# Two attention blocks on one core: reciprocals sent to their rows over DRAM, and a sum of score quarters moved into an earlier phase

## The chip, the core and the metric

The kernel runs on one core of a Trainium2 chip. The engines named below are PE (TensorE, matrix products), DVE (VectorE), ACT (ScalarE), POOL (GpSimd) and SP (SyncE, which issues most of the transfers). The metric is the device time of one execution in microseconds; less is better. The data are float32 throughout.

## The reference

Two layers follow each other on x of shape (8, 512, 32, 32), that is 8 samples of 512 channels and 1024 positions. Layer 0 is attention with 8 heads of 64 channels behind a group norm; layer 1 is attention with one head of 512 channels behind a norm over the whole sample. Cut to what matters:

```python
# layer 0
h = group_norm(x, norm_w, norm_b)
q, k, v = qkv of h, split into 8 heads of 64
attn = softmax(einsum('bhnd,bhmd->bhnm', q, k) / sqrt(64))
o = einsum('bhnm,bhmd->bhnd', attn, v)
x = x + proj_w @ o + proj_b
# layer 1
n = norm of x over a whole sample
q, k, v = wq @ n + bq, wk @ n + bk, wv @ n + bv
attn = softmax(einsum('bci,bcj->bij', q, k) * 512 ** -0.5)
out = einsum('bcj,bij->bci', v, attn)
x = x + wo @ out + bo
```

## The kernel before

The eight samples are computed one after another, each in some 348 us. The order of instructions on PE, ACT and DVE is the order of the program text, written out by hand; the order on POOL and SP is left to the planner of the language. A helper, `at_steps`, runs a generator of matrix products and calls other work (hooks) after its step of a given number, and `together` takes steps from several generators in turn. So a hook's number decides where DVE's work stands in DVE's queue.

Larger matrix products are made by Strassen's scheme in Winograd's form (seven products for eight): `strassen` uses one PSUM bank called `line` and one called `single`, and sums of input quarters with names such as S1 to S4 and T1 to T4. Some products apply the scheme twice.

**Softmax sums of layer 0.** The scores are exponentiated without their maximum. The heads lie two in a tile, so there are four pairs, in the order 0, 2, 1, 3. The sums over keys are gathered in tiles `acc` on DVE (L780). Pairs are joined in couples: couple one is pairs 0 and 2, couple two pairs 1 and 3. After a pair, `fold` moves half of its sums by three transfers (L1039 to L1041). `sum_couple` (L1054) multiplies by ones, so that each head's sum of a half of the positions (g = 0 or 1, 512 positions) stands in a block of 32 partitions, the same number in each. `one_over_couple` (L1065) takes the reciprocals on DVE and sends them to the partitions of their heads: each tile `spreads[pair]` needs, for each half g, the values of two heads on 64 partitions each, so the block of 32 partitions is copied twice for each head. These are eight transfers of 32x512 for each half, issued by SP (L1072). `divide` (L960) multiplies the outputs `o` by the tile. Couple one does this inside the attention of couple two. Couple two does it beside the query and key products of the next sample's layer 0 (`pairs_qk`), by the hooks 3 to 9; behind the last `divide` stand four differences (`combine2`, L1010) and then the projection (`project`, L1163), whose add L1183 empties the bank `single` before PE fills it again. In the last sample the couples are not used; there the rows go by `spread` (L801).

**Scores of layer 1.** The 1024x1024 scores are four quarters of 512x512, C11, C12, C21 and C22; the tile of the quarter in row j and column i of keys and queries is `ps[j][k][i]`, k being which half of its keys. The seven products of the outer scheme are made in three phases:

- phase one: the products that go to several quarters, and P5 (`twice("S1", "T1", ...)`), which is put into `ps[1][k][1]`;
- phase two: `twice("A12", "B21", ...)` on the banks of tag o for C11, beside `twice("S3", "T3", ...)` on the banks of tag s, which completes what C12 and C22 share and puts it into `ps[0][k][1]`;
- phase three: `twice("S4", "B22", ...)` for one quarter and `twice("A22", "T4", ...)` for another.

`twice` applies the scheme a second time inside, so it has seven steps. Each step has two matmuls into the bank `line` or `single`, and an add (or copy) of that bank into a quarter of a tile (L1335 on DVE). A bank is filled again two steps later, and must have been read by then. Steps of the two `twice` of a phase alternate.

Two sums over whole tiles of 128x1024 complete the quarters, both in `with_p5` (L1378): `ps[1][k][0] += ps[1][k][1]` for each k (hooks 14 in phase one and 3 in phase two), and C22, `ps[1][k][1] += ps[0][k][1]`, in `c22(k)`, followed by the exponential (L1299): k = 0 after phase two, k = 1 at hook 3 of phase three. POOL meanwhile makes sums for the values (`sum_v`, L1429), parts of the softmax sums (`add_up`, L1294 and L1296) and second sums for the products of values (`halve_v`, `halve_p`).

Of the kernel before, what the change touches and what calls it, by code (L numbers as in the profile page):

```python
# [37 lines left out]
FP = mybir.dt.float32  # L38
AF = mybir.ActivationFunctionType
ALU = mybir.AluOpType  # L40
# [6 lines left out]
P = 128  # L47
# [4 lines left out]
HALF = 512  # L52
HD = 64
# [12 lines left out]
def two_attention_blocks(  # L66
# [17 lines left out]
    nc = tc.nc  # L84
# [5 lines left out]
    dram = ctx.enter_context(tc.tile_pool(name="dram", bufs=1, space=bass.MemoryType.DRAM))  # L90
# [7 lines left out]
    def banks(tag, name):  # L98
        return psum.tile([P, 2, HALF], FP, tag=tag, name=name)

    def tile2(name):
        return tpool.tile([P, 2, HALF], FP, tag="t", name=name)
# [377 lines left out]
    def sums_b(q, ts, engine=nc.vector):  # L480

        q.update({f"T{i + 1}": t for i, t in enumerate(ts)})
        for n, x, y in [(1, "B12", "B11"), (2, "B22", "T1"), (3, "B22", "B12"), (4, "B21", "T2")]:
            engine.tensor_tensor(q[f"T{n}"], q[x], q[y], ALU.subtract)
        return q
# [101 lines left out]
    def together(*groups):  # L587

        groups = list(groups)
        spares.clear()  # L590
        while groups:
            for g in list(groups):
                if next(g, g) is g:
                    groups.remove(g)
                else:
                    yield
        spares.clear()
# [289 lines left out]
    def layer0(bs, qs, ks, b, norm_next):  # L887
# [24 lines left out]
        accs, sums, invs, spreads = {}, {}, {}, {}  # L912
# [50 lines left out]
        ps = {}  # L963
# [99 lines left out]
            held(ps_couple[g], f"sum_{name}", invs[g])  # L1063

        def one_over_couple(couple, g):  # L1065
            nc.vector.reciprocal(invs[g], invs[g])  # L1066
            for n, pair in enumerate(couple):
                if g == 0:
                    spreads[pair] = tile2(f"inv_{b}_{pair}")
                for j in range(2):  # L1070
                    for r in range(2):
                        nc.sync.dma_start(  # L1072
                            spreads[pair][(j * 2 + r) * 32 : (j * 2 + r + 1) * 32, g, :],
                            invs[g][(n * 2 + j) * 32 : (n * 2 + j + 1) * 32, :],
                        )

        def held_couple(g):
            held(invs.pop(g), f"inv_{b}_{g}")
# [10 lines left out]
        def couple_steps(i):  # L1089
            if ended(i - 1) is not None:  # L1090
                fold(ended(i - 1))
            if ended(i - 5) is not None:
                folded(ended(i - 5))
            couple = couples[0]
            if ended(i - 7) == couple[1]:
                ps_sum = banks("o", f"ps_sum_{b}_{couple[0]}")
                sum_couple(couple, [ps_sum[:, g, :] for g in range(2)])
            for g, (at_copy, at_over, at_held, at_divide) in enumerate([(7, 8, 14, 13), (8, 10, 18, 15)]):
                if ended(i - at_copy) == couple[1]:
                    copy_couple(couple, g)  # L1100
                if ended(i - at_over) == couple[1]:
                    one_over_couple(couple, g)
                if ended(i - at_held) == couple[1]:
                    held_couple(g)
                if ended(i - at_divide) == couple[1]:
                    divide_couple(couple, g)

        last = norm_next is None
        for i in range(2, len(units) + 2):
# [6 lines left out]
            pair, g, kt = units[i - 5] if i >= 5 else (None, None, None)  # L1116
            name = f"0_{b}_{pair}_{g}"
# [8 lines left out]
            pair, g, kt = units[i - 9] if i >= 9 else (None, None, None)  # L1126
            if pair in invs and kt == NT - 1:
                held(invs.pop(pair), f"inv_0_{b}_{pair}_{g}")
            pair, g, kt = units[i - 10] if i >= 10 else (None, None, None)
# [3 lines left out]
        if b == 0:  # L1133
            rows, = throughs
# [3 lines left out]
        if not last:  # L1138


            couple = couples[1]
# [67 lines left out]
    def attention1(xs, norm, b, at_values):  # L1209

        last = b + 1 == B
# [18 lines left out]
        def halve_a(name, t=None, engine=nc.vector):  # L1230
            q = {f"A{n}": v for n, v in halve(q_parts[name], lambda i, j: (j, i)).items()}
            twice_a[name] = sums_a(q, flat(tile2(f"{name}_twice_{b}")) if t is None else t, engine)
# [51 lines left out]
        ps = [[[tile2(f"p_1_{b}_{j}{k}{i}") for i in range(2)] for k in range(2)] for j in range(2)]  # L1284
# [3 lines left out]
        def add_up(j, k, i):  # L1288

            engine = nc.vector if i else nc.gpsimd  # L1290
            for u in range(2):
                seen[i].append(ps[j][k][i][:, u, :])
                if len(seen[i]) == 2:
                    engine.tensor_tensor(acc[:, i, :], *seen[i], ALU.add)  # L1294
                elif len(seen[i]) > 2:
                    engine.tensor_tensor(acc[:, i, :], acc[:, i, :], seen[i][-1], ALU.add)  # L1296

        def exp_of(p):
            nc.scalar.activation(p, p, AF.Exp, scale=norm.factor)  # L1299
# [13 lines left out]
                    nc.scalar.copy(to[:, t % 2, :], bank)  # L1313
                yield

        def twice(a, v, tags, i, j, fresh, final):

            a, v = twice_a[a], twice_b[v]  # L1320
            line, single = (banks(tag, f"ps_{n}_1_{b}_{i}{j}")[:, 0, :] for tag, n in zip(tags, "ls"))

            def multiply(bank, x, y, start):
                for u in range(2):
                    nc.tensor.matmul(  # L1325
                        bank[:, u * 2 * P : (u + 1) * 2 * P], v[y][:, u * P : (u + 1) * P], a[x],
                        start=start and u == 0, stop=True, skip_group_check=True,
                    )

            def at(r, t):  # L1330
                return ps[j][t][i][:, :, r * 2 * P : (r + 1) * 2 * P]

            def add(bank, r, t):
                bank = bank.rearrange("p (u q) -> p u q", u=2)
                nc.vector.tensor_tensor(at(r, t), bank, at(r, t), ALU.add)  # L1335

            def take(bank, r, t):
                if fresh:
                    nc.scalar.copy(at(r, t), bank.rearrange("p (u q) -> p u q", u=2))
                else:  # L1340
                    add(bank, r, t)

            def done(r, t):
                if final:
                    exp_of(at(r, t))
                    if i == 0 and (r, t) in ((0, 1), (1, 0)):
                        add_up(j, t, i)

            multiply(line, "A11", "B11", True)
            take(line, 0, 0)  # L1350
            yield
            multiply(single, "A12", "B21", True)
            add(single, 0, 0)
            done(0, 0)
            yield
            multiply(line, "S2", "T2", False)
            take(line, 0, 1)
            yield
            multiply(single, "S1", "T1", True)
            take(single, 1, 1)  # L1360
            yield
            multiply(line, "S3", "T3", False)
            add(line, 1, 1)
            done(1, 1)
            yield
            multiply(single, "S4", "B22", False)
            add(single, 0, 1)
            done(0, 1)
            yield
            multiply(line, "A22", "T4", False)  # L1370
            take(line, 1, 0)
            done(1, 0)
            yield

        def with_p5(i, j, k):

            to, other = ps[j][k][i], ps[1][k][1] if i == 0 else ps[0][k][1]
            nc.vector.tensor_tensor(to, to, other, ALU.add)  # L1378

        def c22(k):  # L1380
            with_p5(1, 1, k)
            exp_of(ps[1][k][1])


        spare = wpool.tile([P, W_SIZE], FP, tag="w", name=f"spare_{b}")
# [2 lines left out]
        def halve_t3():  # L1388
# [3 lines left out]
            together(  # L1392
                in_turn(together(line(0), line(1)), together(line(2), line(3))),
                twice("S1", "T1", "oo", 1, 1, True, False),
            ),
            {
                2: [lambda: halve_a("A12", spare[0])], 5: [lambda: halve_a("S3", spare[1])],
                8: [halve_t3], 14: [lambda: with_p5(0, 1, 0)],
            },
        )  # L1400
        halve_a("S4", None, nc.gpsimd)
# [29 lines left out]
        for n in range(1, 3):  # L1431
            sum_v(n, nc.gpsimd)
        at_steps(
            together(
                twice("A12", "B21", "oo", 0, 0, False, True), twice("S3", "T3", "ss", 1, 0, False, False)
            ),
            {3: [lambda: with_p5(0, 1, 1)]},
        )
        c22(0)


        twice_v, twice_p = {}, {}
# [8 lines left out]
        def halve_p(name, engine):  # L1451
            q = {
                f"B{i + 1}{j + 1}": p_parts[i][name][:, :, j * 2 * P : (j + 1) * 2 * P]
                for i in range(2) for j in range(2)
            }
            ts = [tile2(f"{name}_p_twice_{b}_{i}") for i in range(2)]
            sums = [t[:, i, :].rearrange("p (u q) -> p u q", u=2) for t in ts for i in range(2)]
            twice_p[name] = sums_b(q, sums, engine)

        if not last:  # L1460
# [2 lines left out]
            together(  # L1463
                twice("S4", "B22", "oo", 0, 1, False, True), twice("A22", "T4", "ss", 1, 0, False, True)
            ),
            {3: [lambda: c22(1)], 5: [] if last else [lambda: halve_p("B22", nc.gpsimd)]},
        )

        for n in range(1, 5):
# [14 lines left out]
        invs, later = [], []  # L1484
# [685 lines left out]
```

## Time and profile before

| | |
|---|---|
| median of 3 runs | 2840.18 us (2839.46 to 2842.13) |
| the profiled execution | 2839.93 us |
| its span, first to last instruction | 2838.1 us |
| granted TensorE clock | 1.000 |
| scores, phases two and three, first sample (334 to 362 us): busy PE, DVE, ACT, POOL | 27.83, 24.05, 11.15, 23.82 us of 28 |
| reciprocal 128x512 on DVE (L1066), 28 times | 3346 ns each |
| sum over 128x1024 in `with_p5` (L1378), 32 times | 1215 to 2158 ns, median 1836 |
| add of a bank into a quarter (L1335) | 683 and 684 ns |
| issue of a transfer of the reciprocals (L1072), 224 times | 507 to 1708 ns, median 589 |
| landing of such a transfer | median 2.0 us |
| write of layer 1's reciprocals to DRAM (L1562), 8 times | issue 550 ns |
| read of them for all partitions (L1564), 8 times | issue 339 ns, landing 3.6 us |

A busy share says how long an engine had an instruction in hand. PE's instructions overlap and their ends are modelled, so PE's share doesn't show short delays; they are read from the starts of its matmuls in order of time. An instruction that waits keeps what stands behind it on its own engine waiting too; so the order on an engine matters as much as its load.

### The profile page before, as it was taken

What the parts mean: (1) busy time and instruction counts of PE and PEld (TensorE: products, weight loads), DVE (VectorE), ACT (ScalarE), POOL (GpSimd) and SP (SyncE); (2) the same over time, 40 slices, a digit from 0 to 9 for tenths busy, and PEclk for the clock granted to TensorE, in tenths of its full rate; (3) what the DMA queues carried; (4) which work ended last, traced back from release to release, by engine and by line L of the source; (5) the groups of instructions that cost most, each with busy time, mean ns of one, the idle gap of its engine ahead of it and who ended that gap; (6) DMA issues with size and microseconds to landing.
All of it is one profiled execution on the core that took longest, in us unless ns stands there. A gap on an engine that the chain in (4) does not pass through costs nothing.

```text
span 2838.1 us, 38370 instructions
## 1 busy us (share of the span) xinstructions
PE 2825.0 (100%) x15328; PEld 1518.4 (53%) x15328; DVE 2124.3 (75%) x2891; ACT 1118.0 (39%) x1564; POOL 273.6 (10%) x236
## 2 busy tenths in 40 slices
PE   9999999999999999999999999999999999999999
PEld 5434765347643476435773356733567335673365
DVE  6686696867867678777777777777777777767867
ACT  3462324623256232553325522265232642326432
POOL 0000220003100040000400004000040000400011
PEclk9999999999999999999999999999999999999999
DMA  8512132121322213213132131322213222121001
GB/s 289 179 42 74 58 121 94 42 89 53 111 93 50 86 70 107 80 46 108 56 108 79 40 106 56 108 79 46 100 59 105 79 56 90 63 85 57 8 16 39
DMA packets 81227, 228.90 MB, mean 81 GB/s; under 512 B 20080, under 2 KB 20880, under 8 KB 74640
## 3 DMA queue, kind: packets, MB, share of 16 engines
q1 hardware_dynamic: 76576, 210.61, 23.0%
q10 hardware_dynamic: 4464, 15.76, 1.7%
q8 instruction: 122, 2.00, 0.3%
q14 instruction: 65, 0.53, 0.1%
HBM read 157.35 MB, written 30.70 MB: 66 GB/s over the span
## 4 chain that ended last, share of the span: by engine, by line
PE 91%; DVE 6%; issue 1%; SPq 1%; DMA 0%; ACT 0%; POOL 0%; DVEq 0%; POOLq 0%
PE s L921 16%; PE ps_o L940 15%; PE ps_q L612 10%; PE ps_v L627 7%; PE ps_o L1489 7%; PE ps_p L612 5%; PE ps_l L1325 4%; PE ps_s L1308 4%; PE ps_k L612 3%; PE ps_l_v L627 3%; PE ps_s L1325 3%; PE ps_l_qk L849 3%; PE ps_s_v L870 2%; PE ps_s_two L1619 2%; PE ps_s_qk L842 2%; PE ps_o_v L870 1%
## 5 line engine op out<-in xcount | busy, mean ns | idle before, releaser
L778 ACT ACTIVATE p<-s 128x1024 f32<-128x1024 f32 x512 | 524.0, 1025 | 322.1 <-PE s L921 308.3
L780 DVE TENSOR_TENSOR acc<-acc,p 128x1024 f32<-128x1024 f32 x384 | 469.2, 1222 | 99.4 <-ACT p L778 86.3
L940 PE MATMUL ps_o<-p,v 64*64 64x512 f32 x4096 | 528.6, 589 | 0.0
L940 PEld LDWEIGHTS ps_o<-p,v 64*64 64x64 f32 x4096 | 156.6, 133 | 282.8 <-issue 278.9
L921 PE MATMUL s<-q,k 64*64 64x512 f32 x2304 | 298.5, 591 | 0.0
L921 PE MATMUL s<-c_q,c_k 64*64 64x512 f32 x1792 | 233.0, 590 | 0.0
L339 POOL TENSOR_TENSOR rstd<-rstd,minus_half 128x4 f32<-128x4 f32 (+1 forms) x16 | 19.8, 1239 | 2087.7 <-DVE rstd L338 2087.7
L921 PEld LDWEIGHTS s<-q,k 64*64 64x64 f32 x2304 | 86.3, 133 | 162.6 <-issue 156.6
L1489 PE MATMUL ps_o<-t_p,s_v 128*128 128x512 f32 x384 | 168.2, 594 | 0.0
L921 PEld LDWEIGHTS s<-c_q,c_k 64*64 64x64 f32 x1792 | 67.7, 133 | 126.3 <-issue 114.9
L780 DVE TENSOR_TENSOR acc<-p,p 128x1024 f32<-128x1024 f32 x64 | 77.9, 1217 | 73.5 <-ACT p L778 73.5
L1299 ACT ACTIVATE p<-p,factor 128x512 f32<-128x512 f32 (+1 forms) x112 | 85.3, 780 | 115.7 <-DVE p L1335 91.2
L1313 ACT COPY p<-ps_s 128x512 f32<-128x512 f32 x96 | 53.1, 588 | 177.1 <-PE ps_s L1308 177.1
L1489 PEld LDWEIGHTS ps_o<-t_p,s_v 128*128 128x128 f32 x384 | 72.3, 190 | 91.3 <-issue 89.2
L1335 DVE TENSOR_TENSOR p<-ps_l,p 128x512 f32<-128x512 f32 x136 | 90.0, 683 | 41.0 <-PE ps_l L1325 40.7
L612 PE MATMUL ps_p<-t_p,w_p 128*128 128x512 f32 x256 | 114.8, 597 | 2.4 <-DVE u_p L1183 1.3
L612 PE MATMUL ps_q<-t,w_wqk 128*128 128x512 f32 x256 | 116.0, 597 | 0.0
L425 ACT COPY u_q<-ps_q 128x512 f32<-128x512 f32 x75 | 43.6, 581 | 177.1 <-PE ps_q L612 177.1
L1066 DVE RECIPROCAL inv<-inv 128x512 f32<-128x512 f32 x28 | 93.7, 3346 | 22.9 <-ACT inv L788 22.9
L425 ACT COPY u_v<-ps_v 128x512 f32<-128x512 f32 x48 | 28.1, 586 | 204.9 <-PE ps_v L627 185.9
L1335 DVE TENSOR_TENSOR p<-ps_s,p 128x512 f32<-128x512 f32 x112 | 74.8, 684 | 37.9 <-PE ps_s L1325 37.9
L627 PE MATMUL ps_v<-w_v,t_again 128*128 128x256 f32 x448 | 99.0, 379 | 0.0
(457 smaller groups left out, 4903.5 us busy)
## 6 DMA issues: line engine op xcount, KB each, us to landing
x<-in_x SPq DMA_DIRECT2D x92, 512.0 KB, 6.8
w_qk<-stored_qk SPq DMA_DIRECT2D x14, 1792.0 KB, 7.3
inv<-inv SPq DMA_DIRECT2D x248, 64.0 KB, 2.0
w_wqk<-stored_wqk SPq DMA_DIRECT2D x8, 1792.0 KB, 7.6
fold<-acc SPq DMA_DIRECT2D x56, 256.0 KB, 3.1
w_wvo<-stored_wvo SPq DMA_DIRECT2D x8, 1792.0 KB, 7.5
out<-x SPq DMA_DIRECT2D x28, 512.0 KB, 3.3
w_v<-stored_v SPq DMA_DIRECT2D x7, 1792.0 KB, 7.1
```

Source lines behind the costliest of these rows:

```text
L612: nc.tensor.matmul(bank, w[a][:, k, c * P : (c + 1) * P], bs[b][:, k, :], start=fresh and k == 0, stop=k == 1, skip_group_check=True,)
L627: nc.tensor.matmul(bank[:, u * 2 * P : (u + 1) * 2 * P], bs[b][:, k, n * P : (n + 1) * P], w[a][:, k, :], start=fresh and u == k == 0, sto ...
L778: nc.scalar.activation(p, s, AF.Exp, scale=factor)
L780: nc.vector.tensor_tensor(acc, first, p, ALU.add)
L921: nc.tensor.matmul(s[cols, j, :], ks[pair][k0 // HALF][rows, k0 % HALF : k0 % HALF + HD], qs[pair][g][rows, :], start=True, stop=True,)
L940: nc.tensor.matmul(o[cols, half, :], vs[kt][rows, c0 : c0 + HD], p[rows, j, :], start=kt == 0, stop=kt == NT - 1,)
L1066: nc.vector.reciprocal(invs[g], invs[g])
L1299: nc.scalar.activation(p, p, AF.Exp, scale=norm.factor)
L1308: nc.tensor.matmul(bank, bs[v][:, k, t * P : (t + 1) * P], q_parts[a][:, k, :], start=a == "A11" and k == 0, stop=k == 1, skip_group_check ...
L1325: nc.tensor.matmul(bank[:, u * 2 * P : (u + 1) * 2 * P], v[y][:, u * P : (u + 1) * P], a[x], start=start and u == 0, stop=True, skip_group ...
L1335: nc.vector.tensor_tensor(at(r, t), bank, at(r, t), ALU.add)
L1489: nc.tensor.matmul(bank, v_parts[kt // 2][a][:, kt % 2, c * P : (c + 1) * P], p_parts[kt // 2][b][:, kt % 2, cols], start=fresh and kt == ...
```

## The change

It has two parts.

In layer 0, each half of a couple's reciprocals is written to DRAM as four rows of 512 (one for each head, from the first partition of each block of 32), and read back by two transfers, one for each pair, which put two rows on 64 partitions each. So there are three transfers for each half in place of eight; the two reads wait for the write to land. Nothing else of `one_over_couple` changes, and its hooks stay.

In layer 1, `c22` no longer sums whole tiles. `twice` gets an argument `also`, called in its inner `done` for each finished quarter; `twice("S3", "T3", ...)` in phase two passes `c22`, which adds that quarter of `ps[0][t][1]` to the same quarter of `ps[1][t][1]` and exponentiates it. So C22 is complete with phase two, as four sums of 128x512 in place of two of 128x1024, and four exponentials in place of two. The sum of the other whole tile (`with_p5(1)`), which must read P5 before C22 is added to it, moves from hook 3 to hook 2 of phase two. In phase three, hook 3 goes, and `halve_p("B22")` on POOL moves from hook 5 to hook 2.

```diff
         def one_over_couple(couple, g):
             nc.vector.reciprocal(invs[g], invs[g])
+            rows = dram.tile([4, HALF], FP, tag=f"inv_{g}", name=f"inv_rows_{b}_{couple[0]}_{g}")
+            nc.sync.dma_start(rows, invs[g][0:P:32, :])
             for n, pair in enumerate(couple):
                 if g == 0:
                     spreads[pair] = tile2(f"inv_{b}_{pair}")
-                for j in range(2):
-                    for r in range(2):
-                        nc.sync.dma_start(
-                            spreads[pair][(j * 2 + r) * 32 : (j * 2 + r + 1) * 32, g, :],
-                            invs[g][(n * 2 + j) * 32 : (n * 2 + j + 1) * 32, :],
-                        )
+                nc.sync.dma_start(
+                    spreads[pair][:, g, :],
+                    rows[n * 2 : (n + 1) * 2, :].unsqueeze(1).to_broadcast([2, HD, HALF]),
+                )
...
-        def twice(a, v, tags, i, j, fresh, final):
+        def twice(a, v, tags, i, j, fresh, final, also=None):
...
             def done(r, t):
+                if also is not None:
+                    also(r, t)
                 if final:
                     exp_of(at(r, t))
...
-        def with_p5(i, j, k):
-            to, other = ps[j][k][i], ps[1][k][1] if i == 0 else ps[0][k][1]
-            nc.vector.tensor_tensor(to, to, other, ALU.add)
-
-        def c22(k):
-            with_p5(1, 1, k)
-            exp_of(ps[1][k][1])
+        def with_p5(k):
+            nc.vector.tensor_tensor(ps[1][k][0], ps[1][k][0], ps[1][k][1], ALU.add)
+
+        def c22(r, t):
+            to, c21 = (ps[j][t][1][:, :, r * 2 * P : (r + 1) * 2 * P] for j in (1, 0))
+            nc.vector.tensor_tensor(to, to, c21, ALU.add)
+            exp_of(to)
...
-                8: [halve_t3], 14: [lambda: with_p5(0, 1, 0)],
+                8: [halve_t3], 14: [lambda: with_p5(0)],
...
-                twice("A12", "B21", "oo", 0, 0, False, True), twice("S3", "T3", "ss", 1, 0, False, False)
+                twice("A12", "B21", "oo", 0, 0, False, True), twice("S3", "T3", "ss", 1, 0, False, False, c22)
             ),
-            {3: [lambda: with_p5(0, 1, 1)]},
+            {2: [lambda: with_p5(1)]},
         )
-        c22(0)
...
                 twice("S4", "B22", "oo", 0, 1, False, True), twice("A22", "T4", "ss", 1, 0, False, True)
             ),
-            {3: [lambda: c22(1)], 5: [] if last else [lambda: halve_p("B22", nc.gpsimd)]},
+            {2: [] if last else [lambda: halve_p("B22", nc.gpsimd)]},
         )
```

## The prediction

> **What bounds the kernel now.** I read the page first, then the order of time on PE, DVE, POOL and SP around the two places that the change touches, in each of the eight samples.
>
> ```profile
> PE 2825.0 (100%) x15328; PEld 1518.4 (53%) x15328; DVE 2124.3 (75%) x2891; ACT 1118.0 (39%) x1564; POOL 273.6 (10%) x236
> ...
> inv<-inv SPq DMA_DIRECT2D x248, 64.0 KB, 2.0
> ...
> inv<-inv_rows SPq DMA_DIRECT2D x8, 512.0 KB, 3.6
> ```
>
> PE is never idle for long. Its 128x512 matmul is two records 0.43 us apart, its 128x256 one two records 0.215 us apart; whenever a record starts later than that, PE was held. I added these delays up: 48 us in the whole span, so no edit that leaves the matmuls alone can bring more. A delay has two parts: the wait, and some 0.107 us after it, because the next group also starts that much late. Only two places concern us.
>
> Place one is the projection of layer 0 (fifth sample, order of time; start and duration in us, in brackets the idle time before and who ended it):
>
> ```profile
> 1629.69 11.84 SPq L1072 DMA_DIRECT2D inv<-inv  x16
> ...
> 1632.10 3.34 DVE L1066 RECIPROCAL inv<-inv 128x512 f32<-128x512 f32 x1
> ...
> 1643.06 0.69 DVE L960 TENSOR_TENSOR o<-o,inv 128x512 f32<-128x512 f32 x1 [1.80 <-DMA inv<-inv]
> ...
> 1646.94 3.23 PE L612 MATMUL ps_p<-t_p,w_p 128*128 128x512 f32 x6 [0.72 <-DVE u_p L1183]
> ```
>
> SP issues sixteen transfers one by one for 11.84 us, the last divide (L960) waits 1.80 us for one of them, and behind it in DVE's order stand four differences (L1010) and the add (L1183) that PE waits for. Wait plus restart at this place and the like one 2 us later, by sample: 0.27, 0.25, 0.24, 0.68, 1.38, 0.75, 1.29; together 4.87 us. The eighth sample divides in another way and is not touched.
>
> Place two is the second and third phase of layer 1's scores (first sample; DVE, POOL and PE in order of time: start, duration, both in us):
>
> ```profile
> 342.15 2.15 DVE L1378 TENSOR_TENSOR p<-p,p 128x1024 f32<-128x1024 f32 x1
> 344.22 1.28 DVE L1335 TENSOR_TENSOR p<-ps_l,p 128x512 f32<-128x512 f32 x2
> ...
> 354.73 2.09 DVE L1378 TENSOR_TENSOR p<-p,p 128x1024 f32<-128x1024 f32 x1
> 356.74 1.27 DVE L1335 TENSOR_TENSOR p<-ps_l,p 128x512 f32<-128x512 f32 x2
> ```
> ```profile
> 339.48 2.50 POOL L1429 TENSOR_TENSOR s_v<-c_v,c_v 128x512 f32<-128x512 f32 x2
> 341.94 3.49 POOL L1429 TENSOR_TENSOR s_v<-s_v,c_v 128x512 f32<-128x512 f32 x2
> ```
> ```profile
> 343.93 1.03 PE L1325 MATMUL ps_s<-spare 128*128 128x256 f32 x4
> 344.95 1.13 PE L1325 MATMUL ps_l<-spare,B_twice 128*128 128x256 f32 x4
> ...
> 356.28 1.03 PE L1325 MATMUL ps_s<-A_twice,T_twice 128*128 128x256 f32 x4
> 357.47 1.13 PE L1325 MATMUL ps_l<-S_twice,B_twice 128*128 128x256 f32 x4 [0.17 <-DVE p L1335]
> ```
>
> A turn of PE (two matmuls, four records) is 0.86 us. Call the turns of the two streams A1, B1, A2, B2 and so on to A7, B7. Each fills a bank that is used again four turns later, so DVE's add of A3 must end before A5 starts. At 343.93 to 344.95 it came 0.16 us late, at 356.28 to 357.47 0.33 us late, both times behind a whole-tile sum of L1378. With restarts: second phase 0.27, 0, 0.26, 0.28, 0.28, 0.27, 0.26 (1.62 us), third phase 0.44 in each of seven samples (3.04 us). The eighth has neither.
>
> **What the Trainium skill says.** (1) "GPSIMD Engine Reference", Specifications: GpSimd shares its SBUF interfaces with VectorE and contends with DVE instructions that have two SBUF inputs. The trace agrees: L1378 takes 1.22 us alone and up to 2.16 beside POOL, the POOL sum then waiting takes 2.27 instead of 1.27, while L1335, which has one input in PSUM, stays at 0.68 to 0.69 beside POOL. (2) "Perfetto Trace Analysis", Optimizing Scalar/DVE Operations: where DVE is not saturated but causes bubbles elsewhere, smaller instructions may finish work sooner. Here the second phase is close to saturated, see below. (3) "DMA: Bandwidth & Descriptors", Anatomy of one DMA: a transfer has a fixed cost of about 2 us, mostly the receipt. Landing of 2.0 us for 64 KB agrees.
>
> **Part 1, reciprocals over DRAM.** Removed: 224 issues at 0.59 us (8 for each of 28 halves). Added: 28 writes of 8 KB, 56 row reads of 256 KB. The trace has the like for layer 1 (write of 4 KB, one read of 512 KB): the read is issued 1.8 us after the write's issue began, its issue takes 0.34 us, and it lands after 3.6. For a half: 0.1 + 1.8 + 2 x 0.34 + at most 3.6 = 6.2 us after its reciprocal; if half the size lands in 2.5, 5.1. Now: the second reciprocal ends at 1635.44, its last row lands at 1643.06, that is 7.6 us (6.5 in the first sample). The last divide then comes at 1640.5 to 1641.6, a lead of 1.4 to 2.5 us in the fifth sample and 0.3 to 1.4 us in the first (242.49 to 249.0 now). The delays to be covered are, without restarts, 0.88 + 0.29 and 0.17, and one restart that falls away moves PE by 0.1. So all are covered, and I take the full 4.9 us. More is excluded, as nothing else of PE hangs on these rows: the rows of the first two head pairs arrive far inside the attention, where no PE delay names them. What is late next is DVE's add of a bank that PE has itself just filled, which has its usual slack. SP waits some 1.1 us for each write (8.6 us for eight in layer 1 now); behind it stands the load of w_wvo, which waits for PE until about the same time anyway. Ends of the cost: -4.9 to 0, should the reads land as late as the rows do now.
>
> **Part 2, C22 by quarters.** Matmuls are the same. DVE loses the two sums at the head of the third phase (1.25 and 2.09 us there) and gets four of 128x512 in the second; the second whole-tile sum comes one add earlier, before B2. Four quarters at 0.68 (L1010: 128x512, two SBUF inputs) are 2.7 us. Load of DVE in the second phase: 14 adds at 0.60 (pairs of them start 1.20 apart; 8.4) + 1.22 + 2.7 = 12.3 us against 14 turns of 0.86 = 12.1, before any wait for POOL. In the third it falls to 8.4 us, so its 3.04 us of delay goes.
>
> The order up to A3's add is now A1, B1, A2, whole sum, B2, first quarter, A3. Zero is the start of A1's add (338.95). A2's add ends at 2.42. The second POOL sum (half of the 2.50 row, so to 3.03) lets the interface go some 0.1 us before its record ends, as the third does now for the whole sum (344.30 - 1.22 = 343.08): 2.95. Whole sum 1.22: 4.17. B2's add: 4.8. Meanwhile the third POOL sum, which waited, has the interface from 4.1 to 5.25 (spacing of these sums 1.23). The first quarter gets it then: 5.9. A3's add: 6.5. A5 starts 0.06 later (as 344.90 to 344.95 now), 6.55. It is due at 5.84 (344.79). Delay 0.71 + 0.107 = 0.81 us. In the second sample POOL runs 0.34 us later: 1.16. In the eighth POOL is silent there: none. Sum 6 x 0.81 + 1.16 = 6.0 us, where now 1.62 stand. Afterwards DVE catches up; following the adds on, A1's add of the third phase ends some 0.1 us before its bank is needed, so I add 0.3 us over all samples. Part 2: 6.0 + 0.3 - 1.62 - 3.04 = +1.6 us. Ends: -4.7 (no delay in either phase) and +10.4 (rival below). The exponentials move with the quarters; ACT is at 11.3 us of 28 in this stretch and nobody on PE's path waits for it.
>
> **Sum.** Against the profiled execution, 2839.93 us (span 2838.1 and 1.8 around it, 0.25 under the median of 2840.18): -4.9 + 1.6 = -3.3, so 2836.6 us.
>
> **Rivals.** *The interface is not in the way* (quarter sum goes ahead of POOL's third sum): A3's add ends at 6.0, delay 0.26 + 0.107, 2.6 us in seven samples; part 2 is -2.1, the time 2832.9; with no delay at all 2830.4. For it: samples in which POOL and DVE met luckily, as the second now. Against: the third POOL sum is already waiting when DVE lets go. *POOL goes first each time* (the slower end): if the waiting third sum precedes the whole sum and the fourth the quarter, A3's add comes 1.35 us later, A5 is 2.16 us late, 15.1 us in seven samples, part 2 +10.4, the time 2845.4. It turns the balance from 1.36 us in each sample on ((4.87 + 4.66) / 7). Against: in each sample now, DVE got in between the third and fourth sum. *Rows no earlier* (the change doesn't do what it says): part 1 at 0, 2841.5. For it: two dependent transfers at about 2 and 3.6 us. Against: the arithmetic above.
>
> **How the numbers follow.** Likeliest 0.46 (own range 2834 to 2839), not in the way 0.30, rows no earlier 0.12, POOL first 0.12. A measurement of this kernel can tell about 0.2% (5.7 us) from no change, so faster means below 2834.3, slower above 2845.6. Faster: 0.9 of the second case, 0.1 of the first, 0.32. Slower: about half of the last, a tenth of the third, 0.07. The range 2831 to 2843 leaves out some 0.05 below and 0.12 above.
>
> **What would show it.** Right: no PE delay at ps_p before L1183; first divides of the second half within 6.2 us of the reciprocal; a delay of 0.7 to 1.1 us at A5 of the second phase, with the whole sum and first quarter both lengthened by POOL; none in the third phase. Wrong: delays at ps_p that stay, or a second phase without a delay, or one above 1.36 us.

## The result, and the profile after

| | before | after |
|---|---|---|
| median | 2841.96 us (6 runs, 2839.46 to 2842.39) | 3042.35 us (6 runs, 3038.61 to 3046.67) |
| ratio after to before | | 1.0708 (1.0695 to 1.0722) |
| span of the profiled execution | 2838.1 us | 3041.2 us |
| granted TensorE clock, mean | 1.000 | 0.975 |

The change makes the kernel 7% slower, far outside the range of the prediction. The page of the changed kernel first: busy time by engine, the clock by fortieths of the span, the chain that ended last, the group of the divides and the issues of the reads.

```profile
PE 2876.4 (95%) x15328; PEld 1532.1 (50%) x15328; DVE 2127.2 (70%) x2907; ACT 1120.9 (37%) x1580; POOL 268.8 (9%) x236
...
PEclk9999999989999899999999999999999998999999
...
PE 79%; DMA 11%; DVE 8%; issue 1%; ACT 1%; SPq 0%; POOL 0%; DVEq 0%; ACTq 0%; POOLq 0%
...
L960 DVE TENSOR_TENSOR o<-o,inv 128x512 f32<-128x512 f32 x64 | 44.0, 691 | 243.2 <-DMA inv<-inv_rows 243.1
...
inv<-inv_rows SPq DMA_DIRECT2D x56, 256.0 KB
```

PE is not busy throughout any more, transfers hold 11% of the chain, and 56 of the 64 divides, instructions of 0.69 us, waited 243.1 us in all for the reads. Which waits reached PE is told by its own waits (waiting line, awaited line, us in total, times, longest).

```profile
PE ps_p L612 <- DVE u_p L1184: 66.4, 7, 10.2
PE s L921 <- ACT p L778: 52.1, 14, 6.0
PE ps_p L612 <- DVE q L644: 32.9, 7, 4.9
PE ps_l L1326 <- DVE p L1336: 3.1, 7, 0.5
```

The first three lines come to 151.4 us. The first and third belong to couple two and stand in the projection; the second, twice in each of seven samples, belongs to couple one, inside the attention. Only the fourth is part 2.

Now one couple, in order of time (start, us, in brackets the idle time before). SP, then DVE, then ACT, couple one of the first sample:

```profile
183.45 0.61 SPq L1069 DMA_DIRECT2D inv_rows<-inv  x1
185.34 1.18 SPq L1073 DMA_DIRECT2D inv<-inv_rows  x2
188.38 0.84 SPq L1069 DMA_DIRECT2D inv_rows<-inv  x1
198.90 1.06 SPq L1073 DMA_DIRECT2D inv<-inv_rows  x2
```
```profile
192.85 0.69 DVE L960 TENSOR_TENSOR o<-o,inv 128x512 f32<-128x512 f32 x1 [0.76 <-DMA inv<-inv_rows]
198.73 0.69 DVE L960 TENSOR_TENSOR o<-o,inv 128x512 f32<-128x512 f32 x1 [5.19 <-DMA inv<-inv_rows]
...
206.84 0.69 DVE L960 TENSOR_TENSOR o<-o,inv 128x512 f32<-128x512 f32 x1 [4.95 <-DMA inv<-inv_rows]
212.18 0.69 DVE L960 TENSOR_TENSOR o<-o,inv 128x512 f32<-128x512 f32 x1 [4.65 <-DMA inv<-inv_rows]
```
```profile
207.62 1.02 ACT L778 ACTIVATE p<-s 128x1024 f32<-128x1024 f32 x1 [8.11 <-DVE o L960]
```

The first half's write needs 1.9 us until its reads go out. Of these two reads, issued together, one lets its divide start 7.5 us and the other 13.4 us after 185.34, so they come one behind the other. The second half's write, issued at 188.38, lets its reads go at 198.90 only, 10.5 us later: just after the last read of the first half has landed. A divide that waits holds DVE, ACT stands idle for 8.11 us until DVE releases its exponential, and PE stands:

```profile
201.67 1.04 PE L940 MATMUL ps_o<-p,v 64*64 64x512 f32 x8
208.69 1.98 PE L921 MATMUL s<-q,k 64*64 64x512 f32 x8 [5.99 <-ACT p L778]
...
214.03 1.99 PE L921 MATMUL s<-q,k 64*64 64x512 f32 x8 [1.65 <-ACT p L778]
```

Eight matmuls take 1.04 us before the wait and 1.98 behind it. The windows give the reason for that, and for the slow reads. Columns: stretch, its length, busy us of PE, PEld, DVE, ACT, POOL (with instructions), granted TensorE clock, mean busy share of the 16 DMA engines, GB/s.

```profile
188.00:192.00 4.00, 4.00 (x44) 1.47 (x40) 3.79 (x4) 2.70 (x5) 0.00 (x0) 1.00 0.14 52
193.00:195.00 2.00, 2.00 (x24) 0.77 (x20) 0.54 (x1) 1.02 (x1) 0.00 (x0) 1.00 0.13 49
415.00:418.60 3.60, 3.60 (x10) 1.69 (x9) 2.79 (x4) 0.58 (x1) 0.00 (x0) 1.00 0.39 146
208.70:214.00 5.30, 3.68 (x16) 0.79 (x16) 1.82 (x3) 1.05 (x2) 0.00 (x0) 0.50 0.09 33
```

While these reads run, 0.13 to 0.14 of 16 engines are busy, that is two, and 49 to 52 GB/s flow: 256 KB then need some 5.1 us (an estimate from these rates), and the divides stand 5.3 and 5.9 us apart. The third row is the read from which the prediction took its 3.6 us, layer 1's 512 KB, in the same kernel: 0.39 of the engines and 146 GB/s. The fourth row is the stretch behind PE's wait: the clock is granted by half.

The account, by the prediction's own method (starts of PE's records against their pace): the delays come to 48.6 us before and 251.7 after, and the difference of 203.1 is that of the spans. In it, single waits of more than 0.6 us grew from 4.5 to 165.6, records at half pace from 6.6 to 50.4 (the clock before was 1.000, so its 6.6 are delays of that size from other causes), and all the rest fell from 37.5 to 35.7.

The page "DMA: Bandwidth & Descriptors" of the Trainium skill, section "Why a DMA increments its semaphore by 16 and not by 1", has the rule that was not applied: the number of engines of a transfer is the largest one, up to 16, that divides the size of the slowest dimension other than 1 on both its sides. The reads' source is written as [2, 64, 512], so two, and the trace agrees with its share of 0.13. The experiments below test it with 4, 16 and 64 in that place.

### The profile page after: what moved, and what is told of

Read it like the earlier page. It is cut to its first block, busy times and chain, and to the rows that moved or that the text cites. A ratio compares the mean times of both kernels' runs of the same rounds, so it can differ in the third digit from the quotient of the medians.

```text
span 3041.2 us, 38101 instructions
## 1 busy us (share of the span) xinstructions
PE 2876.4 (95%) x15328; PEld 1532.1 (50%) x15328; DVE 2127.2 (70%) x2907; ACT 1120.9 (37%) x1580; POOL 268.8 (9%) x236
## 4 chain that ended last, share of the span: by engine, by line
PE 79%; DMA 11%; DVE 8%; issue 1%; ACT 1%; SPq 0%; POOL 0%; DVEq 0%; ACTq 0%; POOLq 0%
PE s L921 12%; PE ps_o L940 11%; PE ps_q L612 9%; PE ps_v L627 6%; PE ps_o L1491 6%; DMA inv<-inv_rows 6%; PE ps_p L612 5%; DMA inv_rows<-inv 4%; PE ps_l L1326 4%; PE ps_s L1309 4%; PE ps_s L1326 3%; PE ps_l_v L627 3%; PE ps_l_qk L849 2%; PE ps_k L612 2%; DVE inv L1067 2%; PE ps_s_v L870 2%
## 5 line engine op out<-in xcount | busy, mean ns | idle before, releaser
L940 PE MATMUL ps_o<-p,v 64*64 64x512 f32 x4096 | 536.5, 597 | 0.0
L921 PE MATMUL s<-c_q,c_k 64*64 64x512 f32 x1792 | 240.8, 608 | 44.4 <-ACT p L778 44.4
L960 DVE TENSOR_TENSOR o<-o,inv 128x512 f32<-128x512 f32 x64 | 44.0, 691 | 243.2 <-DMA inv<-inv_rows 243.1
L612 PE MATMUL ps_p<-t_p,w_p 128*128 128x512 f32 x256 | 128.5, 660 | 66.9 <-DVE u_p L1184 66.4
L612 PE MATMUL ps_p<-o,w_p 128*128 128x512 f32 x192 | 103.1, 679 | 33.3 <-DVE q L644 32.9
L1300 ACT ACTIVATE p<-p,factor 128x512 f32<-128x512 f32 x128 | 89.8, 719 | 111.9 <-DVE p L1336 69.9
L612 PEld LDWEIGHTS ps_p<-t_p,w_p 128*128 128x128 f32 x256 | 53.9, 214 | 140.2 <-DVE u_p L1184 72.4
L425 ACT COPY u_p<-ps_p 128x512 f32<-128x512 f32 x48 | 28.1, 585 | 254.8 <-PE ps_p L612 254.8
```

The lines of the kernel that those rows point to most:

```text
L612: nc.tensor.matmul(bank, w[a][:, k, c * P : (c + 1) * P], bs[b][:, k, :], start=fresh and k == 0, stop=k == 1, skip_group_check=True,)
L921: nc.tensor.matmul(s[cols, j, :], ks[pair][k0 // HALF][rows, k0 % HALF : k0 % HALF + HD], qs[pair][g][rows, :], start=True, stop=True,)
L940: nc.tensor.matmul(o[cols, half, :], vs[kt][rows, c0 : c0 + HD], p[rows, j, :], start=kt == 0, stop=kt == NT - 1,)
```

## The experiments

Two theories of part 1. A: the reads are slow because their outermost dimension of 2 puts them on two engines, where they run one behind the other and later transfers queue behind them. B: they are slow because 64 partitions read the same DRAM row, or because two dependent transfers take that long anyway. Beside that, part 2 could share in the loss. In the first group of experiments the kernel before had a median of 2840.95 us (33 runs), in the second 2840.93 us (48 runs).

### Part 1 alone

The layer 1 edits are undone; the rows go over DRAM as in the changed kernel.

```diff
...
-            {2: [lambda: with_p5(1)]},
+            {3: [lambda: with_p5(0, 1, 1)]},
         )
+        c22(0)
...
```

> Part 1 alone (reciprocals over DRAM in three transfers; scores as before). Theory A (each row read of 2 x 64 x 512 is served by only two of the sixteen DMA engines, so it takes 5 us, and two of them in a row 10 us): 3035 to 3045 us, with some 240 us of DVE waiting at the divides. Theory B (many reads of the same DRAM row are slow whatever serves them): the same. Rival C (the moved sums of the scores are what costs): about 2837 us.

Measured: 3044.15 us, ratio 1.071 (1.0694 to 1.0727), where 3035 to 3045 were expected. The whole loss is part 1.

### Part 2 alone

`one_over_couple` is that of before; the quarters stay.

```diff
-            rows = dram.tile([4, HALF], FP, tag=f"inv_{g}", name=f"inv_rows_{b}_{couple[0]}_{g}")
-            nc.sync.dma_start(rows, invs[g][0:P:32, :])
...
+                for j in range(2):
+                    for r in range(2):
+                        nc.sync.dma_start(
+                            spreads[pair][(j * 2 + r) * 32 : (j * 2 + r + 1) * 32, g, :],
+                            invs[g][(n * 2 + j) * 32 : (n * 2 + j + 1) * 32, :],
+                        )
```

> Part 2 alone (C22 by quarters; rows by eight transfers as before). Theories A and B: 2840 to 2844 us, a delay of 0.7 us at A5 of the second phase in seven samples and none in the third. Rival C: about 3040 us.

Measured: 2842.61 us, ratio 1.0004 (0.9996 to 1.0012), a difference that can't be told from none. The trace of this kernel shows the step that the prediction worked out, DVE and then PE in the second phase of the first sample:

```profile
342.42 1.79 DVE L1380 TENSOR_TENSOR p<-p,p 128x1024 f32<-128x1024 f32 x1
344.13 0.68 DVE L1336 TENSOR_TENSOR p<-ps_s,p 128x512 f32<-128x512 f32 x1
344.84 1.05 DVE L1384 TENSOR_TENSOR p<-p,p 128x512 f32<-128x512 f32 x1
345.81 1.28 DVE L1336 TENSOR_TENSOR p<-ps_l,p 128x512 f32<-128x512 f32 x2
```
```profile
345.06 1.03 PE L1326 MATMUL ps_s<-spare 128*128 128x256 f32 x4
346.54 1.13 PE L1326 MATMUL ps_l<-spare,B_twice 128*128 128x256 f32 x4 [0.46 <-DVE p L1336]
```

The whole sum takes 1.79 us and the first quarter 1.05 while POOL makes its sums; alone they take 1.22 and 0.68. A3's add stands behind them, and A5 starts 0.62 us late, with the restart 0.72. So it is in seven samples, 5.06 us; the third phase has nothing left of its 3.1 us. Against the 4.7 us before in both phases that is +0.4. In the same trace the delays at the projection, which this edit doesn't touch, come to 6.3 us where they were 5.6 (in both sums 0.77 of the eighth sample), so part of the 1.7 us between the medians is scatter.

### Four reads of one row each

Each read is split by head, so that its outermost dimension on both sides is the 64 partitions. Bytes, rows and the two dependent steps are those of the changed kernel; there are four reads for each half in place of two. Part 2 stays. Each row is still read by 64 partitions, so by theory B this kernel should stay slow.

```diff
-                nc.sync.dma_start(
-                    spreads[pair][:, g, :],
-                    rows[n * 2 : (n + 1) * 2, :].unsqueeze(1).to_broadcast([2, HD, HALF]),
-                )
+                for j in range(2):
+                    nc.sync.dma_start(
+                        spreads[pair][j * HD : (j + 1) * HD, g, :],
+                        rows[n * 2 + j : n * 2 + j + 1, :].to_broadcast([HD, HALF]),
+                    )
```

> As the changed kernel, but each read brings one row to 64 partitions (four reads of 64x512 for each half in place of two of 2x64x512; each row is still read 64 times). Theory A: 64 packets go to sixteen engines, a read lands within some 2.5 us, the delays at the projection and in the attention are gone: 2836 to 2839 us. Theory B: as many reads of the same row, so still about 3040 us.

Measured: 2843.7 us, ratio 1.0013 (1.0006 to 1.002). 200 us are gone by the shape of the same reads, so A stands and B falls, but not all the way that was expected. The page's issues (KB, us to landing), the windows, and SP in the first sample at couple two:

```profile
inv<-inv_rows SPq DMA_DIRECT2D x112, 128.0 KB, 3.0
```
```profile
187.00:188.50 1.50, 1.50 (x20) 0.53 (x16) 1.50 (x2) 0.81 (x2) 0.00 (x0) 1.00 0.59 193
```
```profile
242.78 0.52 SPq L1069 DMA_DIRECT2D inv_rows<-inv  x1
244.53 2.37 SPq L1074 DMA_DIRECT2D inv<-inv_rows  x4
```

The engines' share is 0.59 in place of 0.13, and a read lands in 3.0 us. But four issues take 2.37 us: the last goes out at 246.3 and lands at some 249.2, 6.5 us after the reciprocal (its end, 242.75), as late as the rows of before in this sample. PE's delays at the projection are 6.3 us, as in part 2 alone with the rows of before. The issues ate what the landing gained.

### Eight rows, read in four parts

The write takes eight of the partitions (each head's number twice), and the source of each read is [4, 32, 512]: two reads again, the same bytes on the SBUF side, 4 in the outermost dimension.

```diff
-            rows = dram.tile([4, HALF], FP, tag=f"inv_{g}", name=f"inv_rows_{b}_{couple[0]}_{g}")
-            nc.sync.dma_start(rows, invs[g][0:P:32, :])
+            rows = dram.tile([8, HALF], FP, tag=f"inv_{g}", name=f"inv_rows_{b}_{couple[0]}_{g}")
+            nc.sync.dma_start(rows, invs[g][0:P:16, :])
...
-                    rows[n * 2 : (n + 1) * 2, :].unsqueeze(1).to_broadcast([2, HD, HALF]),
+                    rows[n * 4 : (n + 1) * 4, :].unsqueeze(1).to_broadcast([4, 32, HALF]),
```

> As the changed kernel, but eight rows are written (each head's twice) and a read is 4 x 32 x 512. Theory A: four engines with 32 packets of 0.08 us each, 2.6 us for a read, half of now; both reads of a half done about 7 us after the first issue; the second half's write still queues behind the first half's reads: 2860 to 2890 us. Theory B: each row is read 32 times in place of 64, so also about half the time; this run alone does not tell A from B, it gives the slope.

Measured: 2908.01 us, ratio 1.0234 (1.0218 to 1.0249): a third of the loss is left, more than expected. The windows, SP, and PE's longest wait:

```profile
187.00:189.50 2.50, 2.50 (x28) 0.90 (x24) 2.50 (x2) 1.77 (x2) 0.00 (x0) 1.00 0.23 76
```
```profile
188.95 0.60 SPq L1069 DMA_DIRECT2D inv_rows<-inv  x1
194.16 1.10 SPq L1073 DMA_DIRECT2D inv<-inv_rows  x2
```
```profile
PE ps_p L612 <- DVE u_p L1184: 50.3, 7, 7.7
```

0.23 of 16 engines is four, and the second half's reads go out 5.2 us after its write in place of 10.5. The wait halves when the engines double, as A has it. The waits inside the attention are gone; one of some 7.2 us at the projection is left in each of seven samples. The surplus of 18 us over the expectation is about the half clock behind these waits (mean clock 0.989; some 19 us by the starts of PE's records), which had not been counted.

### Thirty-two rows, read in sixteen parts

The same with `rows` of 32 (`invs[g][0:P:4, :]`) and reads of [16, 8, 512].

```diff
-            rows = dram.tile([4, HALF], FP, tag=f"inv_{g}", name=f"inv_rows_{b}_{couple[0]}_{g}")
-            nc.sync.dma_start(rows, invs[g][0:P:32, :])
+            rows = dram.tile([32, HALF], FP, tag=f"inv_{g}", name=f"inv_rows_{b}_{couple[0]}_{g}")
+            nc.sync.dma_start(rows, invs[g][0:P:4, :])
...
-                    rows[n * 2 : (n + 1) * 2, :].unsqueeze(1).to_broadcast([2, HD, HALF]),
+                    rows[n * 16 : (n + 1) * 16, :].unsqueeze(1).to_broadcast([16, 8, HALF]),
```

> As the changed kernel, but 32 rows are written (each head's eight times) and a read is 16 x 8 x 512: three transfers for each half as in the change, only the shape of the read differs. Theory A: a read goes to all sixteen engines; the last row is there 0.1 + 1.8 + 2 x 0.52 + 2.7 = 5.6 us after the reciprocal, one earlier than with four reads: some of the 4.9 us at the projection come back, 2838 to 2842 us. If sixteen rows don't spread: above 2850 us.

Measured: 2838.32 us, ratio 0.9991 (0.9983 to 0.9999), within the 2838 to 2842 that were expected. The page's issues, the windows, then SP and DVE at couple two of the first sample:

```profile
inv<-inv_rows SPq DMA_DIRECT2D x56, 256.0 KB, 3.7
```
```profile
186.00:188.00 2.00, 2.00 (x24) 0.77 (x20) 2.00 (x2) 1.31 (x2) 0.00 (x0) 1.00 0.55 166
```
```profile
242.60 0.51 SPq L1069 DMA_DIRECT2D inv_rows<-inv  x1
244.45 1.16 SPq L1073 DMA_DIRECT2D inv<-inv_rows  x2
```
```profile
239.23 3.34 DVE L1067 RECIPROCAL inv<-inv 128x512 f32<-128x512 f32 x1
...
248.78 0.69 DVE L960 TENSOR_TENSOR o<-o,inv 128x512 f32<-128x512 f32 x1 [0.40 <-DMA inv<-inv_rows]
```

The reads are two again, of 256 KB, and land in 3.7 us. The reciprocal ends at 242.57, and the last divide starts at 248.78: the 6.2 us that the prediction took for the upper end of its landing. PE's delays at the projection fall from 5.6 to 2.0 us. Of the rest, 1.07 us stand in the sixth sample, where the issue of the two reads took 2.08 us in place of 1.16 and the last divide still waited 1.36.

### The first quarter later

Part 2 alone, with `c22(0, 0)` taken out of `also` and put at hook 7, behind B4's add, where POOL's four sums are over. It tests whether POOL at the first quarter makes the 0.72 us.

```diff
-    twice("A12", "B21", "oo", 0, 0, False, True), twice("S3", "T3", "ss", 1, 0, False, False, c22)
+    twice("A12", "B21", "oo", 0, 0, False, True), twice("S3", "T3", "ss", 1, 0, False, False, lambda r, t: (r, t) == (0, 0) or c22(r, t))
...
-            {2: [lambda: with_p5(1)]},
+            {2: [lambda: with_p5(1)], 7: [lambda: c22(0, 0)]},
```

> Part 2 alone, with the first quarter of C22 added after B4 in place of after B2 (rows by eight transfers as before). If the delay of 0.72 us at A5 is the first quarter's sum, queued behind POOL's third sum, in front of A3's add: A3's add ends 0.4 us before A5 is due, no delay in the second or third phase, the kernel 5.0 us below part 2 alone and 4.7 below before: 2835.5 to 2838 us. Rival (DVE simply has 12.3 us of adds for 12.1 us of matmuls in that phase): the delay only moves to a later turn, 2840 to 2844 us.

Measured: 2838.03 us, ratio 0.9991 (0.9982 to 0.9999), at the upper end of the 2835.5 to 2838 that were expected. DVE in the first sample:

```profile
341.90 1.79 DVE L1380 TENSOR_TENSOR p<-p,p 128x1024 f32<-128x1024 f32 x1
...
346.61 0.68 DVE L1384 TENSOR_TENSOR p<-p,p 128x512 f32<-128x512 f32 x1
```

The first quarter is back at 0.68 us; no PE delay is left in the second phase. At the head of the third, where none was expected, stand 0.28 us in each of seven samples, 2.0 us in all, so that of 4.7 us before 2.7 are saved; the medians differ by 2.9. Just ahead of it the last quarter takes 1.14 us on DVE (at 352.37) while POOL has sums in hand; that this makes the 0.28 us was not tested.

### Both mended

Sixteen parts and the late quarter together.

```diff
+            rows = dram.tile([32, HALF], FP, tag=f"inv_{g}", name=f"inv_rows_{b}_{couple[0]}_{g}")
...
+            {2: [lambda: with_p5(1)], 7: [lambda: c22(0, 0)]},
```

> The two mends together (reads over sixteen engines, first quarter after B4). If they add up: 2833 to 2838 us, below before; if reads over DRAM gain nothing at the projection, as late quarter alone.

Measured: 2834.57 us, ratio 0.9977 (0.9968 to 0.9985): faster than the kernel before by 6.4 us, or 0.15 to 0.32%, and within the 2833 to 2838 that were expected. PE's delays fall by 3.4 us at the projection (5.6 to 2.2) and by 2.7 in the scores, 6.1 together.

### Eight transfers from two queues

The other way to shorten SP's sequence: no DRAM, the eight transfers of before, but those of couple two's second pair are issued by ACT's queue, at hooks 5 and 8. With the late quarter.

```diff
+        def rows_of_couple(couple, g, n, queue):
+            pair = couple[n]
+            for j in range(2):
+                for r in range(2):
+                    queue.dma_start(
+                        spreads[pair][(j * 2 + r) * 32 : (j * 2 + r + 1) * 32, g, :],
+                        invs[g][(n * 2 + j) * 32 : (n * 2 + j + 1) * 32, :],
+                    )
...
-                5: [lambda: held_couple(0)],
-                6: [lambda: one_over_couple(couple, 1)],
+                5: [lambda: rows_of_couple(couple, 0, 1, nc.scalar), lambda: held_couple(0)],
+                6: [lambda: one_over_couple(couple, 1, False)],
...
-                8: [lambda: held_couple(1)],
+                8: [lambda: rows_of_couple(couple, 1, 1, nc.scalar), lambda: held_couple(1)],
```

> Late quarter, and the eight transfers of before, of couple two four from SP and four from ACT's queue (issued beside the held copies), none over DRAM. If it is the issue time on one queue that makes the last row late (6.5 to 7.6 us after the reciprocal), it comes at about 5.2 us and the delays of 4.9 us at the projection go: 2830 to 2834 us. If ACT's own work suffers from the issues (0.6 us each): not below late quarter.

Measured: 2844.48 us, ratio 1.0016 (1.0009 to 1.0022): not the 2830 to 2834 us of the first expected case, but the second, in which ACT's own work suffers. ACT, then PE, in the first sample, and PE's waits:

```profile
236.33 2.78 ACTq L1069 DMA_DIRECT2D inv<-inv  x4
239.16 0.63 ACT L788 ACTIVATE held_inv<-inv 128x512 f32<-128x512 f32 x1 [2.77 <-issue]
...
239.79 0.56 ACT L425 COPY u_q<-ps_q 128x512 f32<-128x512 f32 x1
```
```profile
240.41 1.98 PE L612 MATMUL ps_q<-t,w_qk 128*128 128x512 f32 x4 [1.21 <-ACT u_q L425]
```
```profile
PE ps_q L612 <- ACT u_q L425: 6.6, 7, 1.2
```

The projection's delays fall to 2.4 us, so the rows do come earlier. But four issues hold ACT for 2.78 us, the copy of a query bank stands behind them, and PE waits for it 1.2 us at most in each of seven samples: with restarts these query products are delayed by 10.4 us in place of 1.9. The wait was moved to another queue, and PE was nearer to that one. Six of the 21 runs took 2848 to 2850 us; the trace is of one of 2843.84, so what these six had besides stays open.

## Why the prediction was wrong

**Part 1, the step that failed: "and it lands after at most 3.6 us".** The 3.6 us were measured on a read of 512 KB whose source and destination both have 128 outermost. The source of the changed kernel's reads has 2 there. The prediction scaled by bytes ("if half the size lands in 2.5") and took the duration for that of any read from DRAM. By the divides that wait for them, the first read took 7.5 us and the second 13.4; with 4 in the outermost place the loss fell to a third, with 16 the same sum came out at 6.2 us, as the prediction had it at its upper end. So the arithmetic of the dependent steps was right and this one term, taken from a transfer of another shape, was not.

**"SP waits some 1.1 us for each write".** Right for the first half (reads 1.9 us after the write's issue began). For the second it waits up to 9.6 us, because the write stands behind the reads of the first half. The prediction had looked at what stands behind SP's wait and not at what stands ahead of the write on the DMA engines.

**"Ends of the cost: -4.9 to 0".** The upper end was the state of before. It assumed that rows can't come later than eight transfers issued one by one, and nothing excluded that. Likewise, "the rows of the first two head pairs arrive far inside the attention" was true of before, where these divides waited for nothing, but no price was put on rows that come too late for that: 52.1 us of PE's waits are there.

**What followed from a late row had no term at all.** Behind waits of several microseconds the clock was granted by half, 44 us of the 203. The delays that the prediction priced were all below 1 us, and the kernel before, which has them, ran at a clock of 1.000.

**Part 2: held, its size off.** A5 behind the whole sum and the first quarter, both lengthened by POOL, was right; 0.72 us where 0.81 were forecast, 0.72 in the second sample where 1.16 were forecast, none in the eighth, and nothing in the third phase where 0.3 were added. That gives +0.4 by PE's delays in place of +1.6; the experiment alone gives a median 1.7 us higher, with an interval of -1.1 to +3.4. Of the two rivals, a quarter that POOL doesn't delay would have given 0.37 us, and POOL in front of DVE each time 2.16; neither occurred, and the quarter's later place confirmed the mechanism.

**The rivals.** All four cases shared the bound on part 1, so none of them reached the result. "Rows no earlier" was nearest in kind and took the rows to come at the time of before. With part 1 mended by shape alone (sixteen parts), PE's delays changed by -3.6 for part 1 and +0.3 for part 2, and the time by -2.6, which is within the forecast's own range.

## What to carry to other kernels

Before a transfer's duration is taken from another row of the profile, compare the outermost dimension on both sides, not only the bytes, and read off the share of the DMA engines beside it: here reads of the same 256 KB took 3.7 us in sixteen parts and more than 7 in two. For a step that becomes two dependent transfers, list what is ahead of each on the engines as well as what is behind it in the queue, and let the worst case be "later than now", with what then loses its cover. Fewer issues are worth it only if the fewer transfers still spread over the engines: here two reads in 16 parts beat eight transfers, and four reads over 64 partitions each gave it back in issue time.

## What the runs showed of the hardware

- **The spread of a read follows its outermost dimension.** 2, 4, 16 and 64 there, on the DRAM side, gave a busy share of 0.13, 0.23, 0.55 and 0.59 of 16 engines and 49, 76, 166 and 193 GB/s in a stretch inside the reads; for 2 and 4 that is two and four engines. All but the last move the same bytes in the same number of reads. This agrees with the rule of the Trainium skill's page "DMA: Bandwidth & Descriptors" for 2 and 4; the shares for 16 and 64 fit its sixteen engines, but don't prove the number.
- **Transfers on few engines block others.** The second half's write took 10.5 us until its reads went out behind two reads in two parts, 5.2 behind two in four parts, and 2.0 behind two in sixteen (couple one of the first sample; the last issued at 187.84, its reads at 189.85), though the writes grow from 8 to 16 and 64 KB. That the write stands behind the reads on shared engines was concluded from these numbers. The packet records of the changed kernel fit it: from 184 to 199 us they hold twelve packets of 4 bytes, as many as two writes of four rows and two reads in two parts would end with. Two come at 190.0 and 190.1, soon after the second write was issued, and the last four in pairs at 197.7 and 197.8, 198.2 and 198.3: half of the write, read so, passed at once, and half came just behind the second read.
- **Half clock behind waits.** After PE's wait of 5.99 us the clock was 0.50 over the 5.3 us of the stretch shown (a second wait of 1.65 us lies at its end). The skill's page "TensorE: Matmul & The Clock Gate", Part 1, says that an idle window of some 3.4 us halves the clock and a busy one of as much restores it. The trace agrees with the first, and nearly with the second: PE starts again at 265.16 and at 282.01 (first sample, couple two) and has a clock of 0.50 until 269.1 and 286.1, some 4 us each time, and of 1.00 behind that.
- **A wait of 2 us can do it too.** In the last sample of every kernel here PE waits once for 2.0 us (L627), which is shorter than the idle window that the page gives. In six of the ten traces (the changed kernel, part 1 alone, the reads of one row, four parts, both mended, two queues) some 3.4 us at half clock follow; in the other four none do. With the reads of one row the 32 matmuls behind the wait take 8.86 us, in the kernel before 7.17. That is 1.7 us, as much as the medians of part 2 alone and before lie apart.
- **Two SBUF inputs beside POOL.** A DVE sum of 128x512 with both inputs in SBUF took 0.69 us alone and up to 1.14 us beside POOL's sums (part 2 alone, L1384).
